# A recommender's attention over 200 histories: the sixth row-by-row tile in two of three l instead of one, loop bodies of 90 l instead of 45, and a rearranged head

## The chip, the cores and the metric

The kernel runs on one core of one Trainium2 chip. The metric is the device time of one execution in microseconds (us). The time before is a median of 10 runs.

## The reference, cut to what matters

```python
u, it, c = u_emb[user], i_emb[item], c_emb[cate]      # B = 16384 rows of 64 f32 each
h = i_emb[hist]                                       # (L, B, 64), L = 200
feat = concat([h, itb, h - itb, h * itb], -1)         # itb: it for every l
a = dice(feat @ au_W1 + au_b1, au_alpha, axis=1)      # statistics over B, for every l
w = a @ au_W2 + au_b2
cur = sum over l of w * h
z = concat([u, it, c, cur], -1)
z = dice(z @ W1 + b1, alpha1, axis=0)                 # 80 units
z = dice(z @ W2 + b2, alpha2, axis=0)                 # 40 units
return z @ W3 + b3                                    # 2 values per row
# dice(x): p = sigmoid((x - mean) * rsqrt(var + 1e-8)); x * (p + alpha * (1 - p))
```

The bulk of the work is the sum over l: for each of 200 l, 16384 rows of the item table (256 bytes each) are gathered by index, turned so that features lie on partitions, sent through the small attention layer, normalised over the batch, and added into `cur`.

## The kernel before, in words

**Chunks and steps.** A batch of 16384 rows is 128 tiles of 128 rows. Sixteen tiles make a chunk, and eight chunks (ND = 8) make one l. `steps` goes through the chunks one by one with a hand-written order: `step(k)` asks for chunk k's rows, transposes chunk k-1 and starts its layer, evacuates and measures chunk k-2, and weighs chunk k-9 (LAG = 9), whose l has its statistics by then. After the last chunk of an l, `moments` (L402) works out mean, variance and the reciprocal root by `scale_and_shift` (L164).

**Two ways to get rows.** Most tiles of 128 rows come by one indirect DMA that GpSimd issues (`gather`, L125), into one of ROWS = 5 buffers `rows`. In the chunks listed in SIDES = (1, 3, 4, 5, 6, 7), the sixteenth tile comes *by address* instead: `ask` (L302) loads a run of up to LOAD = 24 byte addresses into registers (L314), and then issues one 256-byte DMA per row (L322) into one of three `side` buffers. Half of the rows are issued by SyncE (SP), half by ScalarE (ACT), whose sequencer also runs the activations. Each of the eight steps of an l issues an eighth of the l's rows by address. `place_tile` (L384) waits on the semaphore until 128 rows have landed, and VectorE copies the `side` buffer into the sixteenth place of `rows` (L386); then `transpose` (L153) turns the chunk into `hT`. The transposes are what frees the `rows` buffer for GpSimd.

**Which l have six tiles by address.** Chunk 5 (SOMETIMES) is by address only in some l:

```python
    def has_side(k):
        l, c = divmod(k, ND)
        return c in SIDES and (c != SOMETIMES or l % EACH < MOST)
```

With EACH = 3 and MOST = 1 an l has six tiles by address where l % 3 is 0 and five otherwise. Where chunk 5 is gathered whole, its sixteenth tile needs its own column of indices, which `load_side_ids` (L139) fetches one l ahead. SP's stream has a mark for each l: at chunk 0, `load_hist_ids` (L133) loads the next l's indices; at chunk 2 its addresses follow (L142).

**Loop and rest.** `tc.For_i(0, BODY, LPB)` runs bodies of LPB = 45 l, so that l = 0 to 179 take four trips; all engines meet at the end of a trip. The last 20 l are unrolled after it. There the user's rows are fetched as a further l (`ask_all`, `fetch_all`), and each chunk's `cur` goes into the head as soon as it is complete.

**Prologue and head.** Before the loop the category rows are picked by one-hot matmuls (L500 to L508), the item rows are gathered and the weights laid out. After it come three small layers with batch statistics (`start_moments`, `end_moments`, `dice`, `evacuate`, `finish`, `send`).

The program writes the order out by hand (`manual_schedule`), so each engine's queue follows the order of the calls.

Of the kernel before, what the change touches and what calls it, by code (L numbers as in the profile page):

```python
# [9 lines left out]
I32 = mybir.dt.int32  # L10
# [7 lines left out]
CH = 512  # L18
S = 32
CD = 2 * CH  # L20
LPB = 45
ROWS = 5
LAG = 9
XR = 8
# [1 line left out]
SIDES = (1, 3, 4, 5, 6, 7)  # L26
SOMETIMES = 5
EACH = 3
MOST = 1
LOAD = 24  # L30
SPLIT = 0.5
ROW = 4 * D
# [4 lines left out]
def din_kernel(  # L37
# [109 lines left out]
    def by_tile(t, i):  # L147
        return t[:, ts(i, CH)].rearrange("p (n t) -> p n t", t=S)

    def transpose(dst, of):  # L150
        for i in range(2):
            for e in range(2):
                nc.vector.transpose(by_tile(dst[ts(e, D)], i), of[ts(i, D), :, ts(e, S)])  # L153

    def layer(dst, pairs, first=True, last=True):
        for i in range(2):
# [7 lines left out]
    def scale_and_shift(mean, var, rstd, shift):  # L164

        p, n = mean.shape
        v = small.tile([P, n], F32, tag=f"v{n}", name="v")
        h = small.tile([P, n], F32, tag=f"h{n}", name="h")
        v, h = v[:p], h[:p]
        nc.vector.tensor_scalar_add(v, var, EPS)  # L170
        nc.vector.tensor_single_scalar(h.bitcast(I32), v.bitcast(I32), 1, ALU.logical_shift_right)
        nc.vector.tensor_scalar(
            rstd.bitcast(I32), h.bitcast(I32), -1.0, float(0x5F375A00), ALU.mult, ALU.add
        )
        for _ in range(3):
            if n == 1:
                nc.vector.scalar_tensor_tensor(h, rstd, v, rstd, ALU.mult, ALU.mult)
            else:
                nc.vector.tensor_mul(h, rstd, rstd)
                nc.vector.tensor_mul(h, h, v)  # L180
            nc.vector.tensor_scalar(h, h, -0.5, 1.5, ALU.mult, ALU.add)
            nc.vector.tensor_mul(rstd, rstd, h)
        nc.vector.scalar_tensor_tensor(shift, mean, -1.0, rstd, ALU.mult, ALU.mult)

    blk_h = make("blk_h", P, P)
# [43 lines left out]
    w1a = make("w1a", P, 4, P)  # L229
    w1b = make("w1b", P, 4, S)  # L230
    w2a = make("w2a", P, P)
    w2b = make("w2b", P, 4, P)
    w3 = make("w3", P, 4, P)
    b1a = make("b1a", P, 1)
    b1b = make("b1b", S, 1)
# [9 lines left out]
    def head_weights():  # L245
        for t in (w1a, w1b, w2a, w2b, w3, bias2, al2):
            nc.vector.memset(t, 0.0)
        w1 = W1.rearrange("(f d) z -> d f z", d=D)
        for e in range(2):
            for g in range(2):  # L250
                r, d = quarter(e, g), ts(e, S)
                for f in (slice(0, 2), slice(3, 4)):
                    nc.sync.dma_start(w1a[r, f, ts(g, ZA)], w1[d, f, :ZA])
                    nc.sync.dma_start(w1b[r, f, ts(g, ZB)], w1[d, f, ZA:])
        for g in range(2):

            nc.sync.dma_start(w1a[ts(g, D), 2, ts(g, ZA)], w1[:, 2, :ZA])
            nc.sync.dma_start(w1b[ts(g, D), 2, ts(g, ZB)], w1[:, 2, ZA:])
            nc.sync.dma_start(w2a[ts(g, ZA), g * ZA : g * ZA + Z2], W2[:ZA])
            nc.sync.dma_start(b1a[ts(g, ZA)], col(b1)[:ZA])  # L260
            nc.sync.dma_start(ala[ts(g, ZA)], col(alpha1)[:ZA])
            nc.sync.dma_start(b1b[ts(g, ZB)], col(b1)[ZA:])
            nc.sync.dma_start(bias2[g * ZA : g * ZA + Z2], col(b2))
            nc.sync.dma_start(al2[g * ZA : g * ZA + Z2], col(alpha2))
            for j in range(4):
                r = slice(j * S + g * ZB, j * S + (g + 1) * ZB)
                nc.sync.dma_start(w2b[r, j, g * ZA : g * ZA + Z2], W2[ZA:])
                w = j * S + g * ZO
                nc.sync.dma_start(w3[g * ZA : g * ZA + Z2, j, w : w + ZO], W3)
                nc.sync.dma_start(alb[r], col(alpha1)[ZA:])  # L270
        nc.sync.dma_start(bias3, b3.partition_broadcast(P))
        for t, u in ((ala, al1a), (alb, al1b), (al2, al12)):
            nc.vector.tensor_scalar(u, t, -1.0, 1.0, ALU.mult, ALU.add)

        for t, n in ((same_a, ZA), (same_b, ZB)):
            nc.vector.tensor_single_scalar(lane, lanes, n - 1, ALU.bitwise_and)
            nc.vector.tensor_copy(t, lane)
            nc.vector.tensor_scalar(t, t, 0.0, n / P, ALU.is_equal, ALU.mult)
# [202 lines left out]
    bank = [t[:, ts(i, CH)] for t in (px, ph, pg, wb) for i in range(2)]  # L481

    def order_categories():
        nc.scalar.dma_start(table, c_emb.rearrange("(b p) d -> p b d", p=PB))
        for c in range(ND):
            n, j = TD - (c in SIDES), column(c, 0)
            nc.scalar.dma_start(cs[c][:, :n], columns(r_cate)[:, j : j + n])
            if c in SIDES:
                j = column(c, TD - 1)
                nc.scalar.dma_start(cs[c][:, n:], col(r_cate[j * P : (j + 1) * P]))  # L490

    def spread_categories(q):
        c, i = divmod(q, 2)
# [23 lines left out]
    with tc.manual_schedule():  # L517
        nc.sync.dma_start(ids[0], columns(r_item))
        load_addresses(2, r_item.rearrange("(o b) -> o b", o=1))
        order_categories()  # L520
        load_hist_ids(0, 0)
        load_addresses(0, r_hist[0:1])
# [6 lines left out]
                values[:, b : b + 1], lanes[:, 0:1], -1.0, float(P + b * PB), ALU.mult, ALU.add  # L529
            )  # L530
        scale_addresses(2)
        nc.vector.memset(hm, 0.0)
        for t in (*hT[SPREAD:], *curT[1:]):
            nc.scalar.copy(t, hm)

        for c in range(ND + 1):
# [58 lines left out]
    def end_moments(key, sames):  # L595
        n = len(sames)
        mv = sums[key]
        mean = small.tile([P, n], F32, tag=f"hmean{key}", name="hmean")
        nc.vector.tensor_copy(mean, leading(pg, 0, n))
        dev = small.tile([P, n], F32, tag=f"hdev{key}", name="hdev")  # L600
        nc.vector.tensor_sub(dev, mv[:, :, 0], mean)
        nc.vector.tensor_mul(dev, dev, dev)
        nc.vector.tensor_add(dev, dev, mv[:, :, 1])
        for j, same in enumerate(sames):
            nc.tensor.matmul(leading(wb, j, 1), same, dev[:, j : j + 1], start=True, stop=True)
        rstd = small.tile([P, n], F32, tag=f"hrstd{key}", name="hrstd")
        shift = small.tile([P, n], F32, tag=f"hshift{key}", name="hshift")
        scale_and_shift(mean, leading(wb, 0, n), rstd, shift)
        return [(rstd[:, j : j + 1], shift[:, j : j + 1]) for j in range(n)]

    user, category = ucT[:2], ucT[2:]

    def head_layer(c, pairs, first):
        layer(px, [(w1a[:, f], t) for f, t in pairs], first=first, last=not first)
        layer(ph[:S], [(w1b[:, f], t) for f, t in pairs], first=first, last=not first)

    def evacuate(dst, src, bias, i, j):
        for h in range(2):
# [2 lines left out]

    def head_units(c):
        evacuate(za[c], px, b1a, 0, c)
        nc.scalar.activation(zb[c // 4][ts(c % 4, S)], ph[:S], AF.Identity, bias=b1b)
        if c % 4 == 3:
            for h in range(2):
                measure_head(1, c // 4, zb[c // 4], h)

    with tc.manual_schedule():
# [3 lines left out]
        nc.sync.dma_start(sidx[0], col(r_user[j * P : (j + 1) * P]))  # L633
        first = -(-tiles_by_address(L - BODY)[0] // 3) * 3

        weighed = set(range(-LAG, K - LAG))
        for j in range(ND + 2):
            if j < ND:
                fetch_all(K + j, j, ids[1], u_emb)
# [2 lines left out]
                nc.sync.dma_start(category[j % 2], catT[j])  # L642
            step(K + j, K - 1, weighed)
            weighed.add(K + j - LAG)
            if j >= 2:
                k = max(weighed) + 1
                if k < K:
                    gate(k)
                    weights(k)
                    weigh(k)  # L650
                    weighed.add(k)
            if j < ND:
                ask_all(j, SPLIT, first, NS - 1, U, u_emb)
            if 1 <= j <= ND:
                c = j - 1
                head_layer(c, ((2, category[c % 2]), (1, itT[c]), (3, curT[c])), True)
                if c in SIDES[:-1]:
                    place_tile(K + c, first + SIDES.index(c))
                transpose(user[c % 2], rows[(K + c) % ROWS])
                head_layer(c, ((0, user[c % 2]),), False)  # L660
                head_units(c)

        temps = [y, hm, ucT[2], ucT[3]]
# [12 lines left out]

        pz = [px, ph, pg, wb]
        z2 = itT
        start_moments("z", 0, 2, 0, same_a)
        start_moments("z", 1, 2, 1, same_b)  # L680
        na, nb = end_moments("z", (same_a, same_b))
        ab = ucT[:2]
        for c in range(ND + 2):
            if c < ND:
                dice(curT[c], za[c], na, al1a, ala, 2 if c == 0 else 1)
                layer(pz[c % 4], [(w2a, curT[c])], last=False)
                if c % 4 == 0:
                    dice(ab[c // 4], zb[c // 4], nb, al1b, alb)
                layer(pz[c % 4], [(w2b[:, c % 4], ab[c // 4])], first=False)
            if c >= 2:  # L690
                evacuate(z2[c - 2], pz[(c - 2) % 4], bias2, 2, c - 2)

# [29 lines left out]
        for c in range(ND):  # L722
            g, q = divmod(c, 4)
            dice(curT[c], z2[c], n2, al12, al2, 2 if c == 0 else 1, c % 2 == 1)
            layer(pz[2 * g], [(w3[:, q], curT[c])], first=q == 0, last=q == 3)
            if c == ND - 2:
                finish(0)
                send(0, (nc.sync, nc.sync))
        finish(1)
        send(1, (nc.sync, nc.scalar))  # L730

# [29 lines left out]
```

## Time and profile before

| what | value |
|---|---|
| median of 10 runs | 51300.85 us (51271.0 to 51357.7) |
| the profiled execution | 51283.43 us, its span 51281.6 us |
| TensorE matmul busy | 21760.5 us (42%) |
| GpSimd busy | 23439.1 us (46%) |
| VectorE busy | 15794.8 us (31%) |
| ScalarE busy | 3823.8 us (7%) |
| indirect gathers of the history (L125) | 24400 through `idx`, 133 through `sidx` |
| row DMAs by address (L322) into `side`, from the item table | 68720 by SP, 68624 by ACT |
| mean granted TensorE clock | 0.696 |

"Busy" counts the time in which an engine executes. Instructions that only move registers, wait, or issue a DMA are not busy time: SP, which does nothing else, has no row at all, and ACT's busy time holds its activations alone. What these two queues do is seen in the timeline, where `SPq` and `ACTq` stand for their issuing. A group's line has its busy time, the mean of one instruction in nanoseconds, and the engine's idle time just before it with what ended that.

### The profile page before, as it was taken

Reading aid. Unit: us, or ns where it says so; the run is one execution under the profiler, and the core shown is the slowest. Engines: PE = TensorE matmul, PEld = TensorE weight load, DVE = VectorE, ACT = ScalarE, POOL = GpSimd, SP = SyncE. Lnnn points to the kernel's source line nnn. Section 1 sums busy time; section 2 is a strip of 40 time slices with the busy share of each in tenths; the row PEclk is TensorE's granted clock in tenths of the full one; section 3 lists DMA queues with packets and bytes.
Section 4 is the critical chain, followed back from the end, with each engine's and each line's share of the span. In section 5 each row is a group of like instructions: output and inputs, shape, how many; then the busy total and the mean of one; then the engine's idle time right before and its main releaser. Section 6 shows DMA issues by size and latency. Waiting matters only on the chain. (4 is left out here: it accounts for less than half of the span.)

```text
span 51281.6 us, 428116 instructions
## 1 busy us (share of the span) xinstructions
PE 21760.5 (42%) x39376; PEld 8772.3 (17%) x39376; DVE 15794.8 (31%) x22359; ACT 3823.8 (7%) x3321; POOL 23439.1 (46%) x24783
## 2 busy tenths in 40 slices
PE   3444444444444444443444444444444444444444
PEld 1111111111111111111111111111111111111111
DVE  3333333333333333332333333333333333333333
ACT  0000000000000000000000000000000000000001
POOL 4444444444444444444444444444444444444443
PEclk6667666666676766666666676667666676666677
DMA  1000000000000000001000000000000000000000
GB/s 27 17 17 18 17 17 17 18 18 17 18 17 17 18 17 17 18 17 18 17 18 17 17 18 18 17 17 18 17 18 17 17 17 18 17 17 18 17 17 18
DMA packets 1135481, 907.62 MB, mean 18 GB/s; under 512 B 730703, under 2 KB 730703, under 8 KB 1132425
## 3 DMA queue, kind: packets, MB, share of 16 engines
q0 software_dynamic: 792896, 813.51, 9.0%
q1 hardware_dynamic: 193692, 35.90, 0.4%
q10 hardware_dynamic: 145837, 30.64, 0.3%
q14 instruction: 2746, 22.50, 0.1%
q8 instruction: 310, 5.08, 0.0%
HBM read 873.55 MB, written 4.39 MB: 17 GB/s over the span
## 5 line engine op out<-in xcount | busy, mean ns | idle before, releaser
L125 POOL DMA_INDIRECT rows<-in_L_rec_i_emb,idx x24400 | 23079.6, 946 | 27343.8 <-DVE hT L153 19533.3
L158 PE MATMUL ph<-hT,unit 128*128 128x512 f32 x6404 | 5957.0, 1083 | 23253.6 <-DVE hT L153 22336.7
L367 DVE SCALAR_TENSOR_TENSOR wb<-wb,au_bias,hT 128x1024 f32<-128x1024 f32 x1610 | 2081.2, 1293 | 17332.5 <-remote 11500.1
L158 PEld LDWEIGHTS ph<-hT,unit 128*128 128x128 f32 x6404 | 1781.0, 309 | 26434.2 <-DVE hT L153 25044.1
L158 PE MATMUL wb<-y,blk_p 128*128 128x512 f32 x6440 | 3807.0, 676 | 5618.0 <-DVE y L363 5181.2
L153 DVE STREAM_TRANSPOSE hT<-rows 64x512 f32<-64x512 f32 x6404 | 4516.6, 705 | 366.8 <-DVE rows L386 200.7
L158 PE MATMUL px<-hT,blk_h 128*128 128x512 f32 x6404 | 4063.5, 722 | 300.4 <-ACT xs L371 186.7
L363 DVE TENSOR_TENSOR y<-pg,xs 128x1024 f32<-128x1024 f32 x1610 | 1961.6, 1218 | 7105.8 <-ACT pg L360 6137.3
L371 ACT ACTIVATE xs<-px,au_bias 128x1024 f32<-128x1024 f32 x1602 | 1785.1, 1114 | 25849.5 <-issue 13044.1
L158 PE MATMUL wb<-xs,blk_x 128*128 128x512 f32 x6440 | 3577.1, 639 | 16.8 <-DVE curT L368 16.8
L360 ACT ACTIVATE pg<-xs,sh,rs 128x1024 f32<-128x1024 f32 x1610 | 1943.8, 1207 | 20822.5 <-issue 17836.6
L158 PE MATMUL px<-itT,blk_i 128*128 128x512 f32 x6404 | 3406.0, 614 | 0.0
L158 PE MATMUL px<-hm,blk_m 128*128 128x512 f32 x6408 | 3018.1, 593 | 33.6 <-issue 29.1
L399 DVE TENSOR_TENSOR hm<-ph,itT 128x1024 f32<-128x1024 f32 x1601 | 1959.2, 1224 | 2154.9 <-PE ph L158 1293.9
L158 PEld LDWEIGHTS wb<-y,blk_p 128*128 128x128 f32 x6440 | 1342.0, 215 | 7476.9 <-DVE y L363 5433.3
L386 DVE COPY rows<-side 128x64 f32<-128x64 f32 x1079 | 209.2, 194 | 6920.3 <-DMA side<-in_L_rec_i_emb 6890.1
L376 DVE BATCH_NORM_STATS2 st<-xs 128x6 f32<-128x512 f32 x3204 | 2059.9, 685 | 853.2 <-issue 414.3
L158 PEld LDWEIGHTS px<-hT,blk_h 128*128 128x128 f32 x6404 | 1622.1, 255 | 2774.1 <-issue 2489.0
L368 DVE TENSOR_TENSOR curT<-wb,curT 128x1024 f32<-128x1024 f32 x1610 | 1971.4, 1224 | 54.8
L158 PEld LDWEIGHTS px<-itT,blk_i 128*128 128x128 f32 x6404 | 1395.9, 218 | 1992.0 <-issue 1992.0
L158 PEld LDWEIGHTS wb<-xs,blk_x 128*128 128x128 f32 x6440 | 1320.0, 205 | 1742.4 <-issue 1723.9
L158 PEld LDWEIGHTS px<-hm,blk_m 128*128 128x128 f32 x6408 | 1211.3, 190 | 1590.8 <-issue 1581.4
(177 smaller groups left out, 2084.7 us busy)
## 6 DMA issues: line engine op xcount, KB each, us to landing
side<-in_L_rec_i_emb SPq DMA_DIRECT2D x68720, 0.2 KB
side<-in_L_rec_i_emb ACTq DMA_DIRECT2D x68624, 0.2 KB
rows<-in_L_rec_i_emb,idx POOLq DMA_INDIRECT x24400
idx<-in_r_hist SPq DMA_DIRECT2D x200, 61.0 KB
hT<-cs ACTq DMA_DIRECT2D x16, 500.0 KB
side<-in_L_rec_u_emb SPq DMA_DIRECT2D x336, 0.2 KB
side<-in_L_rec_u_emb ACTq DMA_DIRECT2D x304, 0.2 KB
ucT<-catT SPq DMA_DIRECT2D x8, 512.0 KB
```

Source lines behind the costliest of these rows:

```text
L125: nc.gpsimd.indirect_dma_start(out=dst[:, n, :], out_offset=None, in_=table, in_offset=bass.IndirectOffsetOnAxis(ap=ids, axis=0),)
L153: nc.vector.transpose(by_tile(dst[ts(e, D)], i), of[ts(i, D), :, ts(e, S)])
L158: nc.tensor.matmul(dst[:, ts(i, CH)], lhsT, rhs[:, ts(i, CH)], start=(first and j == 0), stop=(last and j == len(pairs) - 1), skip_group_c ...
L360: nc.scalar.activation(pg, xs[k % XR], AF.Sigmoid, bias=shifts[i], scale=rstds[i])
L363: nc.vector.tensor_mul(y, pg, xs[k % XR])
L367: nc.vector.scalar_tensor_tensor(wb, wb, au_bias2, hT[k % LAG], ALU.add, ALU.mult)
L368: nc.vector.tensor_add(curT[k % ND], wb, curT[k % ND])
L371: nc.scalar.activation(xs[k % XR], px, AF.Identity, bias=au_bias)
L376: nc.vector.bn_stats(stats[l % 3][:, 2 * c + i, :], xs[k % XR][:, ts(i, CH)])
L386: nc.vector.tensor_copy(rows[k % ROWS][:, TD - 1], side[m % 3])
L399: nc.vector.tensor_mul(hm, ph, itT[k % ND])
```

## The change

The constants: LPB goes from 45 to 90, so the loop makes two trips instead of four; MOST goes from 1 to 2, so an l has six tiles by address where l % 3 is 0 or 1. Of 200 l, 134 have six tiles by address instead of 67.

In the statistics, the factor -0.5 is taken into `v` and into the first guess, which takes one VectorE instruction out of each of three Newton steps. In the prologue the category table is loaded after the category indices, and `hm` is cleared ahead of them.

In the end part, `weighed` also holds K and K + 1, so the step that weighed a chunk past the last one (gate, weights, weigh) is gone. The last chunk's user rows are transposed and multiplied in two parts of 12 and 4 tiles. The second layer's small half (`w2b`) keeps one block per row group and is multiplied ahead of the large half, for four or two chunks at a time. `finish(0)` and its `send` come after the last layer's matmuls, not beside them.

```diff
-LPB = 45
+LPB = 90
-MOST = 1
+MOST = 2
...
     def scale_and_shift(mean, var, rstd, shift):
...
-        nc.vector.tensor_scalar_add(v, var, EPS)
+        guess = 0x5F375A00 - (1 << 22) + (1 << 30)
+        nc.vector.tensor_scalar(v, var, EPS, -0.5, ALU.add, ALU.mult)
...
         for _ in range(3):
...
-            nc.vector.tensor_scalar(h, h, -0.5, 1.5, ALU.mult, ALU.add)
-            nc.vector.tensor_mul(rstd, rstd, h)
+            nc.vector.scalar_tensor_tensor(rstd, h, 1.5, rstd, ALU.add, ALU.mult)
...
     def order_categories():
-        nc.scalar.dma_start(table, c_emb.rearrange("(b p) d -> p b d", p=PB))
         for c in range(ND):
...
+        nc.scalar.dma_start(table, c_emb.rearrange("(b p) d -> p b d", p=PB))
...
+        nc.vector.memset(hm, 0.0)
+        nc.scalar.copy(hT[SPREAD], hm)
         order_categories()
...
     def head_units(c):
         evacuate(za[c], px, b1a, 0, c)
-        nc.scalar.activation(zb[c // 4][ts(c % 4, S)], ph[:S], AF.Identity, bias=b1b)
-        if c % 4 == 3:
-            for h in range(2):
+        if c == ND - 1:
+            start_moments("z", 0, 2, 0, same_a)
+        for h in range(2):
+            nc.scalar.activation(
+                zb[c // 4][ts(c % 4, S), ts(h, CH)], ph[:S, ts(h, CH)], AF.Identity, bias=b1b
+            )
+            if c % 4 == 3:
                 measure_head(1, c // 4, zb[c // 4], h)
...
-        weighed = set(range(-LAG, K - LAG))
+        weighed = {*range(-LAG, K - LAG), K, K + 1}
...
-                transpose(user[c % 2], rows[(K + c) % ROWS])
-                head_layer(c, ((0, user[c % 2]),), False)
+                parts = (0, TD) if c < ND - 1 else (0, TD - 4, TD)
+                for n in map(slice, parts, parts[1:]):
+                    transpose(user[c % 2], rows[(K + c) % ROWS], n)
+                    for dst, w in ((px, w1a[:, 0]), (ph[:S], w1b[:, 0])):
...
+        beside = {0: range(4), 4: range(4, 6), 6: range(6, 8)}
         for c in range(ND + 2):
             if c < ND:
-                dice(curT[c], za[c], na, al1a, ala, 2 if c == 0 else 1)
-                layer(pz[c % 4], [(w2a, curT[c])], last=False)
                 if c % 4 == 0:
-                    dice(ab[c // 4], zb[c // 4], nb, al1b, alb)
-                layer(pz[c % 4], [(w2b[:, c % 4], ab[c // 4])], first=False)
+                    dice(ab[c // 4], zb[c // 4], nb, al1b, alb, 2 if c == 0 else 1, c > 0)
+                for i in range(2):
+                    for k in beside.get(c, ()):
+                        r = ts(k % 4, S)
+                        nc.tensor.matmul(
+                            pz[k % 4][:, ts(i, CH)], w2b[r], ab[k // 4][r, ts(i, CH)],
+                            start=True, stop=False, skip_group_check=True,
+                        )
+                dice(curT[c], za[c], na, al1a, ala, 2 if c == 0 else 1, c % 2 == 1)
+                layer(pz[c % 4], [(w2a, curT[c])], first=False)
...
-            if c == ND - 2:
-                finish(0)
-                send(0, (nc.sync, nc.sync))
+        finish(0)
+        send(0, (nc.sync, nc.scalar))
         finish(1)
```

More of the change, by code (lines that the diff above doesn't have):

```diff
@@ L148, in by_tile, with transpose @@
         return t[:, ts(i, CH)].rearrange("p (n t) -> p n t", t=S)
-    def transpose(dst, of):
+    def transpose(dst, of, n=slice(0, TD)):
         for i in range(2):
             for e in range(2):
-                nc.vector.transpose(by_tile(dst[ts(e, D)], i), of[ts(i, D), :, ts(e, S)])
+                nc.vector.transpose(by_tile(dst[ts(e, D)], i)[:, n], of[ts(i, D), n, ts(e, S)])
     def layer(dst, pairs, first=True, last=True):
@@ L169, in scale_and_shift @@
         v, h = v[:p], h[:p]
-        nc.vector.tensor_scalar_add(v, var, EPS)
+        guess = 0x5F375A00 - (1 << 22) + (1 << 30)
+        nc.vector.tensor_scalar(v, var, EPS, -0.5, ALU.add, ALU.mult)
         nc.vector.tensor_single_scalar(h.bitcast(I32), v.bitcast(I32), 1, ALU.logical_shift_right)
         nc.vector.tensor_scalar(
-            rstd.bitcast(I32), h.bitcast(I32), -1.0, float(0x5F375A00), ALU.mult, ALU.add
+            rstd.bitcast(I32), h.bitcast(I32), -1.0, float(guess), ALU.mult, ALU.add
         )
@@ L231, in din_kernel @@
     w2a = make("w2a", P, P)
-    w2b = make("w2b", P, 4, P)
+    w2b = make("w2b", P, P)
     w3 = make("w3", P, 4, P)
@@ L266, in head_weights @@
                 r = slice(j * S + g * ZB, j * S + (g + 1) * ZB)
-                nc.sync.dma_start(w2b[r, j, g * ZA : g * ZA + Z2], W2[ZA:])
+                nc.sync.dma_start(w2b[r, g * ZA : g * ZA + Z2], W2[ZA:])
                 w = j * S + g * ZO
@@ L531, in din_kernel @@
         scale_addresses(2)
-        nc.vector.memset(hm, 0.0)
-        for t in (*hT[SPREAD:], *curT[1:]):
+        for t in (*hT[SPREAD + 1 :], *curT[1:]):
             nc.scalar.copy(t, hm)
@@ L597, in end_moments @@
         mv = sums[key]
-        mean = small.tile([P, n], F32, tag=f"hmean{key}", name="hmean")
-        nc.vector.tensor_copy(mean, leading(pg, 0, n))
+        mean = leading(pg, 0, n)
         dev = small.tile([P, n], F32, tag=f"hdev{key}", name="hdev")
         nc.vector.tensor_sub(dev, mv[:, :, 0], mean)
-        nc.vector.tensor_mul(dev, dev, dev)
-        nc.vector.tensor_add(dev, dev, mv[:, :, 1])
+        if n == 1:
+            nc.vector.scalar_tensor_tensor(dev, dev, dev, mv[:, :, 1], ALU.mult, ALU.add)
+        else:
+            nc.vector.tensor_mul(dev, dev, dev)
+            nc.vector.tensor_add(dev, dev, mv[:, :, 1])
         for j, same in enumerate(sames):
@@ L611, in din_kernel, with head_layer @@
     user, category = ucT[:2], ucT[2:]
-    def head_layer(c, pairs, first):
-        layer(px, [(w1a[:, f], t) for f, t in pairs], first=first, last=not first)
-        layer(ph[:S], [(w1b[:, f], t) for f, t in pairs], first=first, last=not first)
+    def head_layer(pairs):
+        layer(px, [(w1a[:, f], t) for f, t in pairs], last=False)
+        layer(ph[:S], [(w1b[:, f], t) for f, t in pairs], last=False)
     def evacuate(dst, src, bias, i, j):
@@ L644, in din_kernel @@
             weighed.add(K + j - LAG)
[L645 to L651, printed above, removed]
+            left = [k for k in range(K) if k not in weighed]
+            if j >= 2 and left:
+                gate(left[0])
+                weights(left[0])
+                weigh(left[0])
+                weighed.add(left[0])
             if j < ND:
@@ L655, in din_kernel @@
                 c = j - 1
-                head_layer(c, ((2, category[c % 2]), (1, itT[c]), (3, curT[c])), True)
+                head_layer(((2, category[c % 2]), (1, itT[c]), (3, curT[c])))
                 if c in SIDES[:-1]:
                     place_tile(K + c, first + SIDES.index(c))
-                transpose(user[c % 2], rows[(K + c) % ROWS])
-                head_layer(c, ((0, user[c % 2]),), False)
+                parts = (0, TD) if c < ND - 1 else (0, TD - 4, TD)
[4 more added lines that the diff above has]
+                            nc.tensor.matmul(
+                                by_tile(dst, i)[:, n], w, by_tile(user[c % 2], i)[:, n],
+                                start=False, stop=n.stop == TD, skip_group_check=True,
+                            )
                 head_units(c)
@@ L678, in din_kernel @@
         z2 = itT
-        start_moments("z", 0, 2, 0, same_a)
         start_moments("z", 1, 2, 1, same_b)
@@ L682, in din_kernel @@
         ab = ucT[:2]
+        beside = {0: range(4), 4: range(4, 6), 6: range(6, 8)}
         for c in range(ND + 2):
             if c < ND:
-                dice(curT[c], za[c], na, al1a, ala, 2 if c == 0 else 1)
-                layer(pz[c % 4], [(w2a, curT[c])], last=False)
                 if c % 4 == 0:
-                    dice(ab[c // 4], zb[c // 4], nb, al1b, alb)
-                layer(pz[c % 4], [(w2b[:, c % 4], ab[c // 4])], first=False)
+                    dice(ab[c // 4], zb[c // 4], nb, al1b, alb, 2 if c == 0 else 1, c > 0)
+                for i in range(2):
+                    for k in beside.get(c, ()):
+                        r = ts(k % 4, S)
+                        nc.tensor.matmul(
+                            pz[k % 4][:, ts(i, CH)], w2b[r], ab[k // 4][r, ts(i, CH)],
+                            start=True, stop=False, skip_group_check=True,
+                        )
+                dice(curT[c], za[c], na, al1a, ala, 2 if c == 0 else 1, c % 2 == 1)
+                layer(pz[c % 4], [(w2a, curT[c])], first=False)
             if c >= 2:
```

## The prediction

> **What bounds the kernel now.** I read the costliest groups first, then the DMA issues, then SP's own waits, and last the timeline of the queues, since the groups alone mislead here. No engine is busy for half of the span. The group of GpSimd's gathers has more idle time than work, and nearly all of it ends with a transpose on VectorE: GpSimd waits for a free `rows` buffer. VectorE in turn waits for rows that come by address.
>
> ```profile
> L125 POOL DMA_INDIRECT rows<-in_L_rec_i_emb,idx x24400 | 23079.6, 946 | 27343.8 <-DVE hT L153 19533.3
> L386 DVE COPY rows<-side 128x64 f32<-128x64 f32 x1079 | 209.2, 194 | 6920.3 <-DMA side<-in_L_rec_i_emb 6890.1
> side<-in_L_rec_i_emb SPq DMA_DIRECT2D x68720, 0.2 KB
> side<-in_L_rec_i_emb ACTq DMA_DIRECT2D x68624, 0.2 KB
> ```
>
> Does SP, which issues half of those rows, ever rest? Its own waits say no: the largest on a free `side` buffer are these, in us, times, and the longest.
>
> ```profile
> SPq L314 <- DVE rows L386: 108.3, 158, 1.5
> SPq L322 <- DVE hT L153: 12.2, 47, 0.7
> ```
>
> All of SP's listed waits come to some 370 us of 51281.6, and more than half of that lies in prologue and head. So SP issues without a pause through the whole loop. How fast it does so depends on GpSimd. Between gathers SP issued 47 row DMAs in 18.09 us; during a burst of gathers it issued 26 in 37.29 us, and ACT's 20 took 31.96 us there instead of 6.46.
>
> ```profile
> 20018.12 0.95 POOL L125 DMA_INDIRECT rows<-in_L_rec_i_emb,idx  x1 [21.51 <-DVE hT L153]
> 20019.37 0.95 POOL L125 DMA_INDIRECT rows<-in_L_rec_i_emb,idx  x1 [0.30 <-issue]
> ...
> 20000.06 18.09 SPq L322 DMA_DIRECT2D side<-in_L_rec_i_emb  x47
> ...
> 20018.90 37.29 SPq L322 DMA_DIRECT2D side<-in_L_rec_i_emb  x26
> ...
> 20005.33 6.46 ACTq L322 DMA_DIRECT2D side<-in_L_rec_i_emb  x20
> ...
> 20030.47 31.96 ACTq L322 DMA_DIRECT2D side<-in_L_rec_i_emb  x20
> ```
>
> Gathers and row DMAs therefore hardly overlap: the time of an l is about the burst time of its gathers plus the free issue time of its row DMAs. That an l with one tile more by address is longer can be read directly. The line L133 marks each l in SP's stream:
>
> ```profile
> 19619.88 0.36 SPq L133 DMA_DIRECT2D idx<-in_r_hist  x1
> ...
> 19862.96 0.36 SPq L133 DMA_DIRECT2D idx<-in_r_hist  x1
> 19864.92 58.52 SPq L322 DMA_DIRECT2D side<-in_L_rec_i_emb  x80
> 19923.72 0.23 SPq L142 DMA_DIRECT2D addrs<-in_r_hist  x1
> 19925.62 179.75 SPq L322 DMA_DIRECT2D side<-in_L_rec_i_emb  x240
> 20105.84 0.36 SPq L133 DMA_DIRECT2D idx<-in_r_hist  x1
> 20106.42 0.36 SPq L139 DMA_DIRECT2D sidx<-in_r_hist  x1
> 20108.62 61.79 SPq L322 DMA_DIRECT2D side<-in_L_rec_i_emb  x96
> 20170.69 0.23 SPq L142 DMA_DIRECT2D addrs<-in_r_hist  x1
> 20172.76 201.28 SPq L322 DMA_DIRECT2D side<-in_L_rec_i_emb  x288
> 20374.81 0.36 SPq L133 DMA_DIRECT2D idx<-in_r_hist  x1
> ```
>
> Two l with five tiles (80 + 240 = 320 DMAs on SP) last 243.08 and 242.88 us; the l with six (96 + 288 = 384) lasts 268.97. GpSimd starts 123, 123 and 122 gathers in these three stretches, by the windows view, so the two streams go in step. Over all such windows of the loop away from the ends of its trips: six tiles with an index column fetched (l % 3 = 0) 265.05 us, mean of 61; five with a column (l % 3 = 1) 246.39, mean of 57; five without 244.86, mean of 61. The chain of waits is of no use here: its shares add up to some 10% of the span.
>
> **The change part by part.**
>
> *The sixth tile.* 67 l go from five tiles to six. Like with like (both with a column fetched), a tile costs 265.05 - 246.39 = 18.66 us, so 67 x 18.66 = +1250 us. From single instructions: SP issues 64 rows more, each a register move and a DMA that start 0.317 us apart between gathers (20.3 us); the 16 register loads of an l hold 24 addresses instead of 20 (median 1.675 against 1.450 us, +3.6 us); one gather less, 1.25 us from start to start. That is 22.6 us or +1517 in all, my upper bound, since a few of the added rows go out inside a burst at no cost of their own. I take the windows, as they are the whole of what an l pays. ACT gets the same 64 rows and holds its two activations of each step behind them; VectorE gets 67 more waits in `place`, with the transposes, the statistics and the product of that chunk queued behind, and GpSimd waits for those transposes. All of this happens already in the 67 l that have six tiles, and lies in the 18.66.
>
> The same l no longer fetch an index column (L139), 67 times. It takes SP 0.58 us to get past it (20105.84 to 20106.42): -39 us. The two five-tile windows differ by 1.53 us, which would make it -103; I take the smaller, since the first of them also follows a six-tile l.
>
> A rule against this price stands in the Trainium skill, "DMA: Bandwidth & Descriptors", section Issuing engine by pattern: descriptors made by hardware for SP and ACT are generally the faster way. By that, a tile that leaves GpSimd would save at most its 1.25 us here, 84 us in all; the windows above show the opposite for 256-byte rows issued one at a time.
>
> For the longer register loads, the page "Runtime: NRT & Kernel Launch", section Instruction fetch mechanics, gives about 200 ns for each register. Four more would then be 0.8 us a load, an estimate of 67 x 16 x 0.8 = 858 us; this trace has 0.225 us a load, and the windows hold it already.
>
> *Bodies of 90 l.* The ends of trips at l = 45 and 135 go. Around such an end the windows are 192 and 342 us instead of 245 and 265; summed over the nine windows about it, the excess is 12.8, 27.0 and 21.6 us at the three ends inside the loop. Two fewer at their mean of 20.5: -41 us, bounds -26 and -54. The code is twice as long, but each instruction is run through in order as before.
>
> *`scale_and_shift`.* Three VectorE instructions of 0.15 to 0.16 us less in every `moments`, about 0.19 us each from start to start: 0.57 us an l. What hides it is SP's stream, which doesn't wait for VectorE. I take 0; if the statistics were on the path, -114.
>
> *Prologue.* The table's DMA moves behind 14 small ones, which ACT issues until 12.9 us; the first one-hot compare starts at 20.57, the first matmul at 21.43. The copy of `hT` puts an activation ahead of the DMAs on ACT. I take 0, bounds -10 and +13, the length of that series of DMAs.
>
> *End.* The chunk past the last one: its gate, product and weighing lie between the last statistics (done at 51197.05) and `start_moments` (51205.36). Gone, -8.3 us. The four Newton and copy instructions less in each of two `end_moments` at 0.19 us: -1.5. The split transposes let the matmuls on the last user rows start up to three quarters of 2.87 us earlier, -2; `w2b` ahead of the large half hides part of the two cold layers at 51214 to 51220, -4; `finish(0)` after the matmuls instead of beside them, 1.8 us of VectorE and 6 DMAs of 0.43 to 0.46 us each ahead of the last send, +1. Sum -15, bounds 0 and -35.
>
> Sum: 1250 - 39 - 41 + 0 + 0 - 15 = +1155 us. The profiled execution took 51283.4, 17 below the median; 51283.4 + 1155 + 17 = 52455. The bounds of the unknown terms: upper 51301 + 1517 - 39 - 26 + 13 = 52766; lower 51301 + 1250 - 103 - 54 - 114 - 10 - 35 = 52235.
>
> **The rivals.**
>
> *GpSimd is the bound after all, and the kernel gets faster.* Its 24655 history and user gathers are spaced 51282 / 24655 = 2.08 us on average; if that spacing were its own, 67 fewer would be worth -139, with -41 and -15 about 51106 us. For it: each gather stands alone on GpSimd. Against: 19533 us of its idle time end with a transpose, and in a burst it starts one each 1.25 us. It would decide only if SP had slack of more than 18.66 us in a five-tile l, and SP's waits show none. 0.05.
>
> *The step between six and five tiles is half an echo.* SP may run ahead by three `side` buffers, so a window on SP needn't be the time of an l. On VectorE, the products (L399) of an l span 257.9, 250.7 and 247.6 us for l % 3 = 0, 1, 2: the six-tile l is only 8.7 above the mean of the others. At that, 67 x 8.7 = +583, less 95, gives about 51789. Against: VectorE is up to a step behind, so an l's cost smears into the next. 0.08.
>
> *More than the windows say.* Two six-tile l in a row never occur before, and the five-tile l may repair what a six-tile one delays. Counted by their start times, SP starts 42309 row DMAs outside bursts, in 20713 us, 0.49 us each with all loads and the slow ends of bursts. At that price 64 are 31.4 us, and 67 tiles +2101: 53307. Against: the window after a six-tile l is longer by 1.53 us at most. 0.07.
>
> *The edit of MOST reaches no instruction.* `has_side` decides both `fetch` and `ask_hist`, so it moves both; nothing in the code speaks for this.
>
> **How the numbers follow.** The forecast has 0.78, with a range of its own from 52235 to 52766. The other cases need some room at both ends: 52100 to 52850. A measurement can tell 0.2%, about 103 us, from no change. Faster has the 0.05 of the GpSimd case; a near tie needs the second case at a tenth of its size, 0.02; slower has the rest, 0.93.
>
> **What would show it.** In the profile after: row DMAs on SP 73008 (68720 + 67 x 64), 66 fetches at L139's place; SP windows of about 264 to 265, 265 and 245 us for l % 3 = 0, 1, 2; one pair of odd windows inside the loop instead of three; GpSimd's idle time behind the transposes up by about 1200 us; no gate after the last statistics. I am wrong if the second of two six-tile l differs from the first by over 5 us, if five-tile windows shrink, or if SP begins to wait for `side` buffers.

## The result, and the profile after

The changed kernel takes 52511.6 us (median of 8 runs, 52488.4 to 52609.8) beside 51294.6 us before: 1217 us more, a ratio of 1.0239 (95% interval 1.0230 to 1.0248). The forecast was 52455 us, slower, and its own range, 52235 to 52766, holds the result. The profiled execution's span is 52475.7 us, 1194.1 more than before.

First the costliest groups and the DMA issues of the kernel after:

```profile
L125 POOL DMA_INDIRECT rows<-in_L_rec_i_emb,idx x24400 | 23079.5, 946 | 28610.1 <-DVE hT L153 20934.0
L387 DVE COPY rows<-side 128x64 f32<-128x64 f32 x1146 | 221.9, 194 | 9312.5 <-DMA side<-in_L_rec_i_emb 9287.6
side<-in_L_rec_i_emb SPq DMA_DIRECT2D x73008, 0.2 KB
side<-in_L_rec_i_emb ACTq DMA_DIRECT2D x72912, 0.2 KB
```

SP issues the 73008 row DMAs that were forecast. GpSimd's busy time stays where it was, and its idle time grows by 1266 us; what ends with a transpose grows by 1401, and the other idle time falls a little. VectorE waits 2397 us more for rows by address: 67 copies more, and a longer wait for each.

Next SP's own waits after; the columns are us in total, times, longest:

```profile
SPq L315 <- DVE rows L387: 139.1, 191, 1.4
SPq L323 <- DVE rows L387: 10.8, 48, 0.3
```

SP still hardly waits for a free `side` buffer. Is it also SP that VectorE waits for? A tile's 128 rows come partly from SP and partly from ACT, and the order of the code tells which row DMA belongs to which tile. Of VectorE's 901 waits for rows that last over 0.5 us, half end 1.6 us or less after SP had issued its last row of the tile (nine in ten between 1.2 and 2.0 us), while ACT had issued its own last one 39 us earlier (median). Before the change the figures are 1.5 and 36 us. So it is SP's stream that VectorE waits for. The third view is SP's timeline through three l, with the marks of L133:

```profile
19819.74 0.36 SPq L133 DMA_DIRECT2D idx<-in_r_hist  x1
...
20084.12 0.36 SPq L133 DMA_DIRECT2D idx<-in_r_hist  x1
20084.71 0.36 SPq L139 DMA_DIRECT2D sidx<-in_r_hist  x1
20086.89 62.72 SPq L323 DMA_DIRECT2D side<-in_L_rec_i_emb  x96
20149.88 0.23 SPq L142 DMA_DIRECT2D addrs<-in_r_hist  x1
20152.08 194.32 SPq L323 DMA_DIRECT2D side<-in_L_rec_i_emb  x288
20346.92 0.36 SPq L133 DMA_DIRECT2D idx<-in_r_hist  x1
20348.88 58.83 SPq L323 DMA_DIRECT2D side<-in_L_rec_i_emb  x80
20407.98 0.23 SPq L142 DMA_DIRECT2D addrs<-in_r_hist  x1
20409.90 184.67 SPq L323 DMA_DIRECT2D side<-in_L_rec_i_emb  x240
20595.47 0.36 SPq L133 DMA_DIRECT2D idx<-in_r_hist  x1
```

The windows, from one mark of L133 to the next, are 264.4, 262.8 and 248.6 us here. Over all windows away from the ends of trips, the means for l % 3 = 0, 1, 2 are 264.1, 264.4 and 246.3 us (63, 61 and 63 windows); the prediction named 264 to 265, 265 and 245. Three l together take 774.8 us instead of 756.3, 18.5 us for the one tile that was moved, its index column included.

### The profile page after: what moved, and what is told of

The parts are those of the page before. It is cut to its first block, busy times and chain, and to the rows that moved or that the text cites. A ratio compares the mean times of both kernels' runs of the same rounds, so it can differ in the third digit from the quotient of the medians.

```text
span 52475.7 us, 444619 instructions
## 1 busy us (share of the span) xinstructions
PE 21784.2 (42%) x39376; PEld 8778.8 (17%) x39376; DVE 15714.6 (30%) x21812; ACT 3824.9 (7%) x3330; POOL 23375.6 (45%) x24716
## 5 line engine op out<-in xcount | busy, mean ns | idle before, releaser
L364 DVE TENSOR_TENSOR y<-pg,xs 128x1024 f32<-128x1024 f32 x1609 | 1961.0, 1219 | 6982.8 <-ACT pg L361 5569.8
L361 ACT ACTIVATE pg<-xs,sh,rs 128x1024 f32<-128x1024 f32 x1609 | 1942.5, 1207 | 21096.8 <-issue 18768.5
```

What stands on the lines that cost most here:

```text
L361: nc.scalar.activation(pg, xs[k % XR], AF.Sigmoid, bias=shifts[i], scale=rstds[i])
L364: nc.vector.tensor_mul(y, pg, xs[k % XR])
```

## The experiments

The runs came in four series, each on another chip, with the kernel before run alongside. On two chips it took 51316 and 51225 us, as in the recorded result; on the other two 31216 and 31213 us. I call the first two *held up* and the others *free*, for what the traces show below. Since each series had its own chip, the chip and the time of the series can't be told apart as the reason. Every ratio is within one series.

### On a held-up chip: the parts of the change

The changed kernel as it is, and the kernel before as it is, for its profile.

> The changed kernel as it is, beside the kernel before in the same series of runs. In the first series the kernel before took 31216 us instead of 51295, and GpSimd issued gathers without a pause. Theory (two conditions: in the recorded one an instruction on SP or ACT takes 0.7 us during a burst and SP's stream is the bound; in the other the row DMAs hide beside the bursts and GpSimd's 1.25 us a gather is the bound): if before is near 31216 here, after is 67 x 1.25 = 84 us faster for the gathers, about 10 for the loop's ends and 15 for the end part, 31100 us; if before is near 51295, after is near 52510. Rival (the first series had another cause, and the change costs row DMAs in every condition): slower than before by 2% either way.

> The kernel before as it is, for its profile beside the series' times. If it is near 31216 us: gathers 1.25 us apart for the whole of an l, windows of 122 or 123 x 1.25 = 152.5 to 153.8 us, shorter where six tiles come by address; no pairs of instructions of 0.7 us on SP and ACT. If it is near 51295: windows of 265, 246 and 245 us again.

After: 52522.0 us against 51316.0, ratio 1.0233 (1.0219 to 1.0247). Before, one run: 51387.3, with windows of 264.9, 247.1 and 245.5 us. Both repeat the recorded times.

The kernel before, with the constant alone changed:

```diff
-MOST = 1
+MOST = 2
```

> The kernel before with MOST = 2 alone (bodies of 45 l, the old end part). With before near 51295: +67 x 18.4 less 67 columns at 0.6 us, 52490. With before near 31216: 67 gathers less at 1.25 us, 31132 us; rival there: ACT, with 384 row DMAs at 0.31 us, its loads and its activations (some 165 us for an l of six), comes to bound, and two l in three at about 160 us give 31700 or more.

52605.2 us, +1289, ratio 1.0246 (1.0232 to 1.0260); windows 264.5, 264.8 and 246.4. That is 1289 / 67 = 19.2 us a tile, where the interval of the ratio reaches from 17.8 to 19.9; the expectation comes to 17.8. By the windows a tile costs some 18 us here too.

The changed kernel without it:

```diff
-MOST = 2
+MOST = 1
```

> The changed kernel with MOST = 1: bodies of 90 l, the shorter statistics and the rearranged head, without the sixth tile's change. With before near 51295: two ends of trips (-41) and the end part (-15), 51240. With before near 31216: 31190, the two ends at 8 us each and the end part at 15 to 20.

51262.6 us, -53, ratio 0.9990 (0.9981 to 0.9999). All the rest of the change, the 90-l bodies and the end part foremost, is worth about a tenth of a per cent, and -41 - 15 = -56 were forecast for it. The two parts add to +1236, and together they measured +1206. So the sixth tile accounts for the whole loss.

### On a free chip: fewer tiles by address, and the change once more

Four versions of the changed kernel, from five tiles by address in every l down to one. Five tiles need the first column of indices ahead of the loop:

```diff
-MOST = 2
+MOST = 0
...
         load_hist_ids(0, 0)
+        load_side_ids(0, 0)
```

The others set MOST = 3, so that all l are alike, and name the chunks:

```diff
-SIDES = (1, 3, 4, 5, 6, 7)
+SIDES = (1, 3, 5, 7)      # four; (3, 7) for two, with SOMETIMES = 3; (7,) for one, with SOMETIMES = 7
```

> The changed kernel with five tiles by address in every l: 134 tiles fewer than after, 200 columns fetched. Theory (row DMAs and gathers share the time of an l, and SP's stream is the bound): windows of about 246 us for every l; 134 x 18.4 us less than after's 52512, plus 134 columns at 0.6 us, is 50125 us. Rival (GpSimd comes to bound as it gets more gathers back): no less than before, about 51250 or more.

> The changed kernel with four tiles by address in every l (chunks 1, 3, 5, 7): 800 instead of 1134. Theory, at 18.4 us a tile: 52512 - 334 x 18.4 = 46370 us, windows of about 228 us. Rival (the price holds only next to five or six, and GpSimd's gathers set the end below): the fall stops near the five-tile time, 50100.

> The changed kernel with two tiles by address in every l (chunks 3 and 7): 400 instead of 1134. Theory, at 18.4 us a tile: 52512 - 734 x 18.4 = 39010 us. Rival (a floor by GpSimd and the work that gathers hold up): the curve flattens and stays above 43000. The gathers' bursts alone, 126 x 1.25 us, would be 157 us an l, 32300 us with prologue and end.

> The changed kernel with one tile by address in every l (chunk 7): 200 instead of 1134. Theory: 52512 - 934 x 18.4 = 35330 us, with another bound (gathers, 127 x 1.25 us = 159 us an l, or TensorE with 150 us an l of matmuls and weight loads) about to take over. Rival: flat from two tiles on, or slower than with two.

With five tiles 31280.2 us (ratio 1.0020, 1.0008 to 1.0032, to the 31216.1 of before), with four 31446.9 (1.0074), with two 31934.0 (1.0230), with one 32175.3 (1.0307). Each theory had been written for a chip like the recorded one, and none of its times came; from five tiles down the kernel gets slower, not faster. The trace of five tiles shows why: first GpSimd's gathers one after another, then their group, then ACT's row DMAs in the same stretch.

```profile
15006.14 0.95 POOL L125 DMA_INDIRECT rows<-in_L_rec_i_emb,idx  x1 [0.30 <-issue]
```

```profile
L125 POOL DMA_INDIRECT rows<-in_L_rec_i_emb,idx x24400 | 23086.5, 946 | 7540.2 <-issue 7163.1
```

```profile
15010.08 6.87 ACTq L323 DMA_DIRECT2D side<-in_L_rec_i_emb  x20
```

GpSimd issues a gather each 1.25 us nearly without a pause (idle 7540 us, nearly all of it the 0.30 between two gathers). ACT issues 20 row DMAs during this burst in 6.87 us, against 31.96 in a burst on the chip of the recorded result. Counted over the records of both queues, row DMAs that took over 0.5 us are 12.8% there before the change and 0.2% here. On the free chip row DMAs and gathers overlap, and GpSimd is the bound, as the rivals of five tiles and of one had it: from five tiles to one, 800 gathers more cost 895 us, 1.12 each.

Does the change, which takes gathers away, then gain on a free chip? In a second such series:

> The changed kernel as it is, once more, for a series in which the kernel before is near 31216 us: 31100 us there if GpSimd's gathers are the bound (67 x 1.25 = 84 us less, some 25 for loop ends and end part), 31700 or more if ACT's 384 row DMAs an l come to bound in the six-tile l. Near 51300 for before: 52515 again.

31881.9 us against 31213.4, ratio 1.0214 (1.0197 to 1.0231): +669 us, the case with 31700 or more. The 31100 us of c1_after_again for such a chip was wrong, and the 2% that its rival named came. SP's marks stand as follows:

```profile
15149.50 0.36 SPq L133 DMA_DIRECT2D idx<-in_r_hist  x1
...
15288.69 0.36 SPq L133 DMA_DIRECT2D idx<-in_r_hist  x1
15290.87 37.35 SPq L323 DMA_DIRECT2D side<-in_L_rec_i_emb  x96
15328.50 0.23 SPq L142 DMA_DIRECT2D addrs<-in_r_hist  x1
15330.58 126.71 SPq L323 DMA_DIRECT2D side<-in_L_rec_i_emb  x288
15457.81 0.36 SPq L133 DMA_DIRECT2D idx<-in_r_hist  x1
```

A five-tile l takes 139.19 us, and the six-tile l after it 169.12. Over all windows away from the ends of trips the means for l % 3 = 0, 1, 2 are 168.6, 161.4 and 137.2, so 155.7 us an l. GpSimd makes 367 gathers in three l; at 1.25 us they need 152.9 us an l. What holds it up are, in VectorE's and in GpSimd's waits of this run:

```profile
DVE rows L387 <- DMA side<-in_L_rec_i_emb: 1084.6, 154, 15.5
```

```profile
POOL rows L125 <- DVE hT L153: 533.5, 143, 7.6
```

With five tiles the same two lines read 31.5 us and 0.6 us. ACT's timeline shows where the late rows come from:

```profile
15067.20 1.11 ACT L372 ACTIVATE xs<-px,au_bias 128x1024 f32<-128x1024 f32 x1 [12.01 <-PE wb L158]
15068.99 7.96 ACTq L323 DMA_DIRECT2D side<-in_L_rec_i_emb  x24
15076.99 1.21 ACT L361 ACTIVATE pg<-xs,sh,rs 128x1024 f32<-128x1024 f32 x1 [8.68 <-issue]
15078.88 7.81 ACTq L323 DMA_DIRECT2D side<-in_L_rec_i_emb  x24
15086.80 1.11 ACT L372 ACTIVATE xs<-px,au_bias 128x1024 f32<-128x1024 f32 x1 [8.60 <-DVE wb L368]
```

A step of a six-tile l fills ACT for 19.6 us without a pause (15067.20 to 15086.80), 157 us in eight steps, over the 152.5 of that l's gathers even before ACT waits for anything. No run separated ACT from SP, but the trace does: of VectorE's 149 waits for rows over 0.5 us, 141 fall in six-tile l, and they end 5.0 us after ACT's last row of the tile and 42 us after SP's (medians of all). It is the other way round from the chip of the result. So the change is slower here too, for another reason: a six-tile l holds more than ACT can issue in the time of its gathers.

Half of the gathers, in the same series, from the kernel with five tiles (the line added for the first column is there too); half of the history's rows are left out:

```diff
-        for n in range(TD - has_side(k)):
+        for n in range(0, TD - has_side(k), 2):
```

> Five tiles by address in every l, as in e4_five, but each chunk of the history fetches only every other of its gathered tiles (8 of 15 or 16); the rest of the rows buffer keeps old rows, so half of the history's rows are left out. 64 gathers an l instead of 123, row DMAs unchanged. If before is near 51300 in this series, theory (bursts and free issuing add up): a gather less is 1.25 us of burst less, in which SP issued 1.1 rows that now cost 0.385 us each outside, 0.82 us net; 59 x 200 x 0.82 = 9700 us less than five tiles' 50125, about 40400 us. Rival (GpSimd's gathers only wait and are off the path): near 50100. If before is near 31216: GpSimd is no longer the bound, and ACT (320 row DMAs at 0.31 us, 16 loads, 19 us of activations) or TensorE (150 us an l) is, at some 150 us an l, 30700 us against five tiles' 31280.

29286.6 us, 1994 less than five tiles in the other free series; the windows fall from 153.5 to 143.1 us. GpSimd now waits 12993 us for transposes and is no longer the bound, as expected; the next one lies at 143 us an l, lower than the 150 I gave it. Of ACT and TensorE it is TensorE by the profile's chain of waits, which has 39% of the span on TensorE's matmuls, 12% on VectorE and next to nothing on ACT. The held-up chip's forecast wasn't tested by it.

### On another held-up chip: the two theories that were left

Two tiles by address, the kernel of e6_two:

> Two tiles by address in every l (chunks 3 and 7), as in e6_two, for a series in which before is near 51300 us. Theory there, at the 18.4 us a tile of the windows: 52512 - 734 x 18.4 = 39010 us, far under both kernels. Rival (the bursts hold up every engine, so more gathers bring their own cost): above 43000. If before is near 31216: 31934 again, GpSimd at 126 x 1.25 us an l.

42207.9 us against 51224.5, ratio 0.8242 (0.8226 to 0.8259). Fewer row DMAs are worth much here: (52522 - 42208) / 734 = 14.1 us a tile, with the kernel after taken from the other held-up chip. But 39010 isn't reached: the price falls on the way from six tiles to two. Two groups of this run show what is left:

```profile
L125 POOL DMA_INDIRECT rows<-in_L_rec_i_emb,idx x25200 | 23798.8, 944 | 17812.4 <-DVE hT L153 10056.9
L364 DVE TENSOR_TENSOR y<-pg,xs 128x1024 f32<-128x1024 f32 x1609 | 1961.8, 1219 | 12115.9 <-issue 10284.8
```

A window is 207.5 us, and 126 gathers take 157.5; GpSimd waits some 50 us in each l for transposes (10057 / 200). VectorE waits 10285 us ahead of L364 for nothing that the profile names. SP is no longer the bound: it waits 2207 us for addresses and 1492 for `side` buffers. What holds VectorE up is seen in one burst, in ACT's timeline and then VectorE's:

```profile
20023.42 25.72 ACTq L323 DMA_DIRECT2D side<-in_L_rec_i_emb  x15
20049.20 1.21 ACT L361 ACTIVATE pg<-xs,sh,rs 128x1024 f32<-128x1024 f32 x1 [25.98 <-issue]
```

```profile
20050.44 1.23 DVE L364 TENSOR_TENSOR y<-pg,xs 128x1024 f32<-128x1024 f32 x1 [17.52 <-issue]
```

L364 needs the gate of L361, and ACT runs that gate behind 15 row DMAs, which took 25.72 us in the burst; 16 between bursts took 5.13. All 786 waits over 3 us ahead of L364, 12096 us together, end within 0.3 us of a gate's end, and 783 of these gates follow a row DMA as closely. The same kernel on the free chip idles 20.7 us there. So with two tiles it is ACT's row DMAs in the bursts that delay VectorE. Its next transposes come after this product in the order of the code, which would explain what GpSimd waits for; no run took the row DMAs off ACT to try it.

More rows to SP, fewer to ACT:

```diff
-SPLIT = 0.5
+SPLIT = 0.53
-LOAD = 24
+LOAD = 26
```

> The changed kernel with SPLIT = 0.53 and LOAD = 26: of 96 rows a step SP issues 51 and ACT 45 (48 and 48 before), of 80 rows 42 and 38; item and user rows shift a little too. If before is near 31216 us in this series, theory (ACT, with its activations behind 384 row DMAs, is the bound of six-tile l there): ACT's six-tile l falls by 24 x 0.31 = 7.4 us to some 159, the mean of three l below GpSimd's 122.33 x 1.25 = 153 us, so GpSimd is the bound again and the time 31110 us, under before and after. Rival (SP or the landing of the rows is the bound of the six-tile l): 31880 or more. If before is near 51300, theory (SP's stream alone is the bound): 64 rows more on SP in three l at 0.317 us, 200 / 3 x 20.3 = +1350, 53870 us. Rival (both queues share one slow stream): 52515.

57652.3 us, ratio 1.1259 (1.1241 to 1.1278), some 5130 over the kernel after (again that of the other held-up chip) where 1350 were expected. The sign fits SP's stream as the bound, but the run doesn't prove it, for something else came in with it. The register loads of this run, and then of the kernel after on the chip of the result (shortest, median, longest in ns):

```profile
L315 ACTq TENSOR_LOAD <-addrs x3295: 3/4906/5711, 19.1 to 57499.3; - x194
L315 SPq TENSOR_LOAD <-addrs x3238: 3/1980/5758, 3.3 to 57512.1; - x191
```

```profile
L315 ACTq TENSOR_LOAD <-addrs x3295: 3/1665/5648, 19.5 to 52347.4; - x194
L315 SPq TENSOR_LOAD <-addrs x3238: 3/1591/4817, 3.4 to 52361.0; - x191
```

There are as many loads, but ACT's median is three times as long, and SP's total more than twice. The code tells where in the list of addresses each load starts. Loads that start on a multiple of four addresses stay short (medians of 1.89 us for 25 addresses, 1.67 for 21), those that start elsewhere take 5.53 us for 26, 4.43 for 21, 4.30 for 19 and 5.18 for 23. All loads together grow from 4393 to 10348 us on SP and from 4960 to 15053 on ACT. SP's loads alone grow by more than the unexplained 3800 us; part of that falls into bursts, in which SP then has fewer slow row DMAs (11.6% over 0.5 us instead of 13.4%). SP still waits for nothing longer than 1.9 us in the loop, and VectorE's waits for rows still end right after SP's last row (median 1.3 us), 36 us after ACT's. So the trace has SP's stream as the bound in this run as well. ACT's loads do show: VectorE's waits for the gate grow from 5570 to 12550 us. A run with more rows on SP and short loads wasn't made.

## Why the prediction was right

**The tile's price.** +1250 us were forecast for 67 tiles from the windows of before. By the windows of after a moved tile costs 18.5 us with its column, 67 x 18.5 = 1240, where the prediction had 1250 - 39 = 1211. The edit alone measured 1289, 19.2 a tile; the instructions' own sum, 22.6, was indeed an upper bound. Two six-tile l in a row cost what one cost, so reading the price from the l that had six tiles already was sound. That SP is the bound, which the prediction read from SP's few waits, is borne out by VectorE's waits, which end with SP's last row before and after.

**Too strong.** "Gathers and row DMAs therefore hardly overlap" says more than the numbers do: by the prediction's own count 42309 of SP's 68720 rows start outside bursts, so 38% of them go out within. The bursts slow the row DMAs; they don't shut them out. The price from the windows doesn't rest on that sentence.

**The column.** -39 us was perhaps too much by about 20: the six-tile windows after differ by 0.3 us with and without one (264.4 and 264.1), 67 x 0.3 = 20. They also differ in their place, first or second of two.

**Bodies of 90, end and prologue.** The profile has 101.2 us from the last user transposes to the end before, and 86.9 after (52388.8 to 52475.7): -14.3 for -15. The first window, which holds most of the prologue, is 4.7 us longer, where I took 0 in bounds of -10 to +13; but from execution to execution this window varies more than that (427 and 447 us in the two profiles of before), so the term isn't resolved. The end of a trip at l = 90 that stays costs 25.7 and 13.7 us over plain windows in the two held-up profiles of after, so -41 for the two that went is of the right size. With tiles, these give 1240 - 41 - 14 + 5 = 1190, against 1194 between the profiled spans. That it fits so closely is in part luck: of two profiles of the same kernel, before or after, the spans are 104 and 46 us apart.

**The rivals.** That half of the step between six and five tiles is an echo, 8.7 us a tile, falls with the edit alone: 19.2. That there is more than the windows say, 31.4 us a tile, falls too. That GpSimd is the bound and the kernel gets faster is false on the chip of the result. On a free chip its premise holds for the kernel with five tiles, and the kernel after is still slower by 2.1%, since ACT's late rows in the six-tile l make VectorE, and so GpSimd, wait.

**What the prediction didn't see.** It took the slow issuing in bursts as part of the kernel. The same kernel on another chip is without it, 20000 us faster, and there the path of the prediction isn't the path at all. The forecast is right for the chips of its profile, and its mechanism holds there alone. On a free chip the direction comes out as forecast, but by ACT's queue and not by SP's: for such a chip it would have been luck. The rule of the Trainium skill on register loads that the prediction set aside ("Runtime: NRT & Kernel Launch", section Instruction fetch mechanics, about 200 ns a register) does hold for loads that don't start on a multiple of four addresses: 5.53 us / 26 = 0.21 us. For those of the kernel before and after, 1.675 us / 24 = 0.07, the trace decided rightly.

No kernel here was seen to beat both on both kinds of chip. On a held-up chip two tiles by address are 18% faster than before, and on a free one 2.3% slower; the changed kernel with MOST = 1 is faster by a tenth of a per cent on a held-up chip and wasn't run on a free one.

## What to carry to other kernels

Where a kernel already does in some iterations what a change does in more of them, compare those iterations in the trace: the price read there includes every wait, and it beat the sum of the instructions. Work that is moved from one queue to another is cheap only up to the point where the new queue's busiest iteration outlasts the old one's, as ACT's 157 us did GpSimd's 152.5 here. Where a wait ends with "issue", look at what the other engine did just before: the gate behind ACT's row DMAs was found so. When two queues seem to exclude each other, run the kernel on a second chip before believing that this belongs to the kernel.

## What the runs showed of the hardware

- The kernel before took 51316 and 51225 us on two chips and 31216 and 31213 on two others. While GpSimd issues gathers, instructions on SP and ACT can take some 0.7 us each on the first two, register moves too. For the kernel after, 11.9% of the row DMAs and 11.2% of the register moves ahead of them took over 0.5 us on the chip of the result, 0.6% and none on a free one. TensorE's granted clock was 0.691 and 0.808 in these two traces, but the median row DMA of SP took the same 0.23 us in both, so it is the bursts that differ. The cause wasn't tried.
- An indirect gather of 128 rows of 256 bytes takes 1.25 us from start to start for the whole of an l on a free chip, while 128 rows by address, 64 on each queue at some 0.31 us, keep two queues busy for about 20 us.
- Loading 26 addresses into registers took 5.53 us where the first of them wasn't at a multiple of four addresses, and 25 took 1.89 us where it was.
